# A transformer block with spline weights: gate and up products from 48 features per sorted row group instead of 256-sample rows

## The chip, the cores and the metric

One core of one Trainium2 chip runs the whole program. The metric is the device time of one execution, in microseconds, as the median of several runs. One further execution is taken with the hardware profiler; the figures of the profile are of that one. PE is the matrix engine (PEld its weight loads), DVE the vector engine, ACT the activation engine, POOL the general engine, and SP the engine that issues most of the transfers (DMA); SPq is its queue in the views.

## The reference

Sixteen sequences of 256 tokens with 256 channels go through one pre-norm block: attention with 16 heads of 16, masked so that a token sees no more than 16 tokens ahead, and then a gated feed-forward part with 1024 inner rows. All in float32.

```python
x = x + attn(layernorm(x), wq, wk, wv, wo)
h = layernorm(x)
gate = einsum('bsh,ih->bsi', h, spline(gate_cp, 1024, 256))
up = einsum('bsh,ih->bsi', h, spline(up_cp, 1024, 256))
x = x + einsum('bsi,hi->bsh', silu(gate) * up, spline(down_cp, 256, 1024))
```

`spline` lays 2033 control points evenly over the 262144 entries of the weight in row order and interpolates them with a cubic (Catmull-Rom): each entry is a sum of four neighbouring control points with factors that are a cubic in its place between two knots. A knot comes about every 129 entries, so a half row of 128 entries holds at most one knot: on each side of it the entries are one cubic.

## The kernel before

The kernel is a software pipeline over the 16 sequences. Its outer loop (`for s in range(B + 4)`, from L790) runs 20 steps; in step s several sequences are in work at once: projections of s+3, maxima of the scores of `nb` = s-1, exponentials and values of `tb` = s-2, output projection and second norm of `ob` = s-3, and the feed-forward part of s-4. The engines are wrapped in `InOrder` (L78), so each engine executes its instructions in the order in which the program writes them. All instructions carry the line of that wrapper, L88, in the profile, so they are told apart by tile name.

A step goes, in program order: `inner` (scores of one group of four heads: into PSUM, exponentials by ACT, row maxima by DVE as `z`, `mx`); `values` of `ob`'s second half (tile `po`, copied by ACT to `au`) and `gather`; a second `inner`; `invert`; projections; `outer`; a third `inner`, `values` of `tb`'s first half; `divide`; a fourth `inner`; `project_o` (py); `stats_f`; `outer`; `norm_f` (xnf); `turn_f`; `turn_max`. The pieces of the feed-forward part of s-4 (`gate_up` 0 to 3, `down` 0 and 1) are put between these by `fill(s, gap)` (L697).

Softmax is divided late. `gather` (L517) sends the sums of exponentials from `au` to `den` (four transfers) and half of the heads to `ac` (four). `invert` (L535) takes the reciprocal on DVE (`rec<-den`), writes it to a DRAM tile `rd`, sends the other half of the heads (four transfers), and reads `rd` back spread over 128 partitions as `rb` (two transfers). `divide` (L551) multiplies `ac` by `rb` on DVE, and `project_o` needs it. `turn_max` (L486) turns the maxima on PE (pm), copies them to `mxT` on ACT and sends them into the query tile `qk` (four transfers) for the scores of the next step. `spread` (L337) sends the projected queries and keys into `qk` (eight transfers), `send_factors` and `spread_factors` (L301, L306) send the norm's factors through DRAM (`ra`, `fa`), `load_x` and `load_xT` load inputs, `down` (L618) sends `out`. Nearly all of these leave from SP, which also takes its work in program order and waits at each transfer for what that transfer needs.

Gate and up weights are dense, turned tiles `gateT` and `upT` (128 x 2 x 1024). They are made in the first four steps by `coefficients` (L648, DVE) and `spline` (L655: four PE products, two ACT copies and two predicated DVE copies for each of six parts; two of these parts are `downT`). `turn_f` (L575) turns the normed `xnf` into `x2T`, with 16 DVE transposes of 32-row blocks, for the first and the last sequence on PE. `gate_up(b, i)` (L599) makes 256 inner rows: per weight 2 x 2 products of 128x128 by 256 tokens, for i = 0 and 3 or 0 and 2 (by step) cut in 32-column pieces. PSUM tiles for these come from the pool `ps_f` with two buffers of one bank, so that gate and up products of one piece are two tiles (`pg`, `pu`). ACT makes tanh of the gate (`th`), DVE does `(th + 1) * gate` and then `inter = th * up`.

Of the kernel before, what the change touches and what calls it, by code (L numbers as in the profile page):

```python
# [11 lines left out]
F32 = mybir.dt.float32  # L12
# [64 lines left out]

class InOrder:  # L78
# [15 lines left out]
def block_kernel(  # L94
# [8 lines left out]
    cps: bass.AP,  # L103
    tab: bass.AP,
# [14 lines left out]
    sbx = ctx.enter_context(tc.tile_pool(name="sbx", bufs=10))  # L119
    dr = ctx.enter_context(tc.tile_pool(name="dr", bufs=2, space=bass.MemoryType.DRAM))  # L120
    ps_s = ctx.enter_context(tc.tile_pool(name="ps_s", bufs=1, space=PSUM))
    ps_f = ctx.enter_context(tc.tile_pool(name="ps_f", bufs=2, space=PSUM))
# [30 lines left out]
    cp_in = sb1.tile([P, 8, S], F32, tag="inter", name="cp_in")  # L153
    cp_in = cp_in.rearrange("p i s -> p (i s)").rearrange("p (w n) -> p w n", n=NPART)
    second_in = const.tile([P, 2, NROW], mybir.dt.uint8, tag="second", name="second_in")
    sp.dma_start(cp_in[:, 0, :], cps[0])
    sp.dma_start(second_in, second)
    load_x(2)

    def load_rest(_):  # L160

        load_x(3)
        sp.dma_start(cp_in[:, 1, :], cps[1])
        load_x(4)
        sp.dma_start(cp_in[:, 2, :], cps[2])
        load_x(5)
        load_weight("o", woT, sp)

# [32 lines left out]
    def constants():  # L201

        for t, n, first in ((mask0, JB, 0), (mask1, S, P)):
            pool.memset(t, 0.0)
            pool.affine_select(
                out=t, in_=t, compare_op=ALU.is_ge, fill=NEG, base=first + LOOK,
                pattern=[[-1, n]], channel_multiplier=1,
            )

    gateT = const.tile([P, 2, INTER], F32, tag="gateT", name="gateT")  # L210
    upT = const.tile([P, 2, INTER], F32, tag="upT", name="upT")
    downT = const.tile([P, 8, DIM], F32, tag="downT", name="downT")


    xns, mxs, aus, aos, recs, x2s, x2Ts = ({} for _ in range(7))
# [70 lines left out]
    def sum_weights(nm):  # L286
        sums[nm] = ps_f.tile([P, DIM], F32, tag="f", name=f"sum{nm}")
        for kc in range(2):
            pe.matmul(
                sums[nm], lhsT=means, rhs=w_in[nm][:, kc, :], start=(kc == 0), stop=(kc == 1)  # L290
            )
# [19 lines left out]
    def project_part(b, i, home="m"):  # L311

        if i == 0:
            qkcs[b] = sb.tile([P, 2, 2, S], F32, tag="qkc", name=f"qkc{b}")
        nm, qkc = "qk"[i], qkcs[b]
        pq = (ps_m if home == "m" else ps_f).tile([P, 2, S], F32, tag=home, name=f"p{nm}{b}")
        for oc in range(2):
            for kc in range(2):
                pe.matmul(
                    pq[:, oc, :],  # L320
                    lhsT=w_in[nm][:, kc, oc * P : (oc + 1) * P],
                    rhs=xTs[b][:, kc, :],
                    start=(kc == 0),
                    stop=(kc == 1),
                )
        if b < RAW:
            act.copy(qkc[:, i], pq)
        else:
            dve.tensor_tensor(
                qkc[:, i], pq, across[b].unsqueeze(1).to_broadcast([P, 2, S]), ALU.mult  # L330
            )

# [14 lines left out]
    def project_v(b, engine=act, chunks=(0, 1), home="m"):  # L347
# [3 lines left out]
        else:  # L351
            pv = (ps_m if home == "m" else ps_f).tile([P, 2, DIM], F32, tag=home, name=f"pv{b}")
# [222 lines left out]
    def turn_f(b):  # L575
        x2Ts[b] = sb.tile([P, 2, S], F32, tag="x2T", name=f"x2T{b}")
        if b in (0, B - 1):

            transposed(x2s.pop(b), x2Ts[b], f"tf{b}")
            return  # L580

        src = x2s.pop(b).rearrange("p c (kc d) -> p c kc d", kc=2)
        dst = x2Ts[b].rearrange("p kc (c t) -> p c kc t", c=2)
        for m in range(0, P, 32):
            for q in range(0, P, 32):
                dve.transpose(
                    dst[m : m + 32, :, :, q : q + 32], src[q : q + 32, :, :, m : m + 32]
                )

    def product(out, lhsT, rhs, start, stop, columns=P):  # L590

        for at in range(0, P, columns):
            pe.matmul(
                out[at : at + columns], lhsT=lhsT[:, at : at + columns], rhs=rhs,
                start=start, stop=stop,
            )


    def gate_up(b, i, columns=P):  # L599
        if i == 0:  # L600
            inters[b] = sb1.tile([P, 8, S], F32, tag="inter", name=f"inter{b}")
        pp = []
        for nm, w in (("g", gateT), ("u", upT)):
            t = ps_f.tile([P, 2, S], F32, tag="f", name=f"p{nm}{b}_{i}")
            for ic in range(2):
                for kc in range(2):
                    at = (2 * i + ic) * P
                    product(
                        t[:, ic, :], w[:, kc, at : at + P], x2Ts[b][:, kc, :], kc == 0, kc == 1,
                        columns,  # L610
                    )
            pp.append(t)
        th = sb.tile([P, 2, S], F32, tag="th", name=f"th{b}_{i}")
        act.activation(th, pp[0], AF.Tanh, scale=0.5)
        dve.scalar_tensor_tensor(th, th, 1.0, pp[0], ALU.add, ALU.mult)
        dve.tensor_tensor(inters[b][:, 2 * i : 2 * i + 2, :], th, pp[1], ALU.mult)

    def down(b, c):  # L618
        inter = inters[b]
        if (b, c) == (B - 1, 1):  # L620

            for n in range(0, DIM, P):
                at = slice(n, n + P)
                pd = ps_f.tile([P, P], F32, tag="f", name=f"pd{b}_{c}_{n}")
# [8 lines left out]
        pd = ps_f.tile([P, DIM], F32, tag="f", name=f"pd{b}_{c}")  # L633
# [14 lines left out]
    def coefficients(w):  # L648

        dve.scalar_tensor_tensor(  # L650
            cp_in[:, w, :], cp_in[:, w, :], 0.5 if w == 2 else 1.0, tab_in[:, 0:NPART],
            ALU.mult, ALU.mult,
        )

    def spline(w, part, home="ffmm"):  # L655
        at = slice(NPART * part, NPART * part + NPART)
        places = tab_in[:, NPART + P * part : NPART + P * part + P]

        pw = [

            tiles[q // 2][:, q % 2, :]
            if tag == "s"
            else (ps_f if tag == "f" else ps_m).tile(
                [P, NPART], F32, tag=tag, name=f"pw{w}_{part}_{q}"
            )
            for q, tag in enumerate(home)
        ]
        for q in range(4):
            rows = slice(32 * q, 32 * q + 32)
            pe.matmul(  # L670
                pw[q], lhsT=places[rows], rhs=cp_in[rows, w, :], start=True, stop=True
            )
        for kc in range(2):
            first, other, where = pw[2 * kc], pw[2 * kc + 1], second_in[:, kc, at]
            if w < 2:
                to = (gateT, upT)[w][:, kc, at]
            else:

                to = downT[:, kc::2, NPART // 4 * part : NPART // 4 * (part + 1)]
                first, other, where = (  # L680
                    t.rearrange("p (o q) -> p q o", q=4) for t in (first, other, where)
                )
            act.copy(to, first)
            dve.copy_predicated(to, where, other)

# [4 lines left out]
    parts = ((0, 0), (1, 0), (0, 1), (1, 1), (2, 0), (2, 1))  # L690

    def keep_running(n):
        run = ps_f.tile([P, 2 * S], F32, tag="f", name="run")
# [3 lines left out]
    def fill(s, gap):  # L697

        if s < B - AHEAD:
            order = (  # L700
                (1, gate_up, 0, 32), (3, gate_up, 1), (4, gate_up, 2, 32), (5, gate_up, 3),
                (6, down, 0), (7, down, 1),
            )
        else:
            order = (
                (1, gate_up, 0, 32), (2, gate_up, 1), (3, gate_up, 2), (4, gate_up, 3, 32),
                (6, down, 0), (7, down, 1),
            )
        for at, stage, *what in order:
# [3 lines left out]


    def part(i, home="ffmm"):
        spline(*parts[i], home)

    early = {
        (0, 1): ((stats_a, 1), (value_ones, 1)),
        (0, 2): (  # L720
            (norm_a, 1), (project_qk, 0), (spread, 0), (load_rest, 0), (coefficients, 0),
        ),
        (0, 4): (
            (turn_a, 1, dve), (project_v, 0, dve, (0, 1), "s"), (stats_a, 2), (norm_a, 2),
            (project_part, 1, 0, "f"), (part, 0, "fmmf"),
# [4 lines left out]
        (1, 2): ((project_part, 2, 0), (coefficients, 1)),  # L730
# [4 lines left out]
        (1, 5): ((part, 1),),  # L735
        (1, 6): ((project_qk, 3),),
        (1, 7): (
            (spread, 3), (stats_a, 4), (stats_a, 5), (part, 2, "ssss"), (norm_a, 4),
# [4 lines left out]
            (project_part, 4, 0), (turn_a, 5), (coefficients, 2), (stats_a, 6),  # L743
            (scores_and_values, 5),
        ),
        (2, 3): ((project_part, 4, 1), (spread, 4), (project_part, 5, 0)),
        (2, 4): ((norm_a, 6),),
        (2, 5): ((project_part, 5, 1),),
        (2, 6): ((project_v, 3, act, (1,)), (project_v, 4)),
        (2, 7): ((part, 3, "ssss"), (part, 4)),  # L750
        (3, 1): ((turn_a, 6),),
        (3, 2): ((project_part, 6, 0), (sum_weights, "q"), (center, "q")),
        (3, 3): (
            (project_part, 6, 1), (sum_weights, "k"), (sum_weights, "v"), (center, "k"),
            (center, "v"),
        ),

        (3, 4): ((spread, 5), (spread, 6)),
        (3, 6): ((project_v, 6), (project_v, 5, act, (0,))),
        (3, 7): ((part, 5, "ssss"), (project_v, 5, act, (1,))),  # L760
    }

    def project(s, gap):
# [3 lines left out]
        for stage, b, at in (  # L767
            (stats_a, pb + 1, 1),
            (project_qk, pb, 2),
            (spread, pb, 2),  # L770
            (send_factors, pb + 1, 2),
            (load_xT, pb + 1, 4),
            (project_v, pb, 6),
# [16 lines left out]
    for s in range(B + 4):  # L790
# [36 lines left out]
        if 0 < ob < B - 1:  # L827
            turn_f(ob)
        fill(s, 6)
        if ob == B - 1:  # L830
            turn_f(ob)
        project(s, 6)
        if tb == B - 1:
            values(tb, 1)
            gather(tb)
        do(turn_max, nb)
        project(s, 7)
        if ob == 0:
            turn_f(ob)
        fill(s, 7)  # L840
# [30 lines left out]
```

## Time and profile before

| | us |
|---|---|
| median of 3 runs (646.12 to 646.79) | 646.13 |
| span of the profiled execution | 643.4 |
| a step with projections (s = 4 to 12) | 37.6 |
| a step without (s = 13 to 16) | 32.5 |
| the last three steps together | 80.4 |

| engine operation, tile | count | busy us | mean ns of one |
|---|---|---|---|
| PE products pg and pu | 2560 records | 245.5 | 380 |
| PE products pd | 528 | 117.4 | 376 |
| PE products scores | 4096 | 106.1 | 317 |
| DVE maxima z, with the read of the accumulator | 512 + 512 | 154.4 + 42.7 | 363 + 83 |
| DVE stream transposes x2T | 224 | 67.8 | 303 |
| DVE th and inter | 64 + 64 | 44.0 + 44.0 | 688 |
| ACT tanh th | 64 | 38.3 | 598 |

The span of the profile is the time from the first to the last instruction; the device time holds 2.7 us more. A float32 product of 128 rows by 256 columns leaves two records on PE, and products on different parts of the array overlap, so the busy time of a group is less than its count times its mean. A step is measured between the first score products of two `inner` calls that follow each other at its beginning.

### The profile page before, as it was taken

How to read it: one execution, taken by the hardware profiler on the slowest of the kernel's cores; microseconds unless marked ns; L12 is line 12 of the kernel's file. 1: busy time of each engine (PE TensorE's matmuls, PEld its weight loads, DVE VectorE, ACT ScalarE, POOL GpSimd, SP SyncE). 2: the span in 40 equal slices, each digit the busy share in tenths (PEclk: the TensorE clock that was granted, in tenths of full speed). 3: DMA queues.
4: the chain of work that ended last, by engine and by line, in shares of the span. 5: the costliest groups of instructions: out<-in, count | busy, mean ns of one | idle time of the engine just before them, and what ended most of it. 6: DMA issues, size and time to landing. Idle time of an engine off the chain costs nothing.

```text
span 643.4 us, 21632 instructions
## 1 busy us (share of the span) xinstructions
PE 631.0 (98%) x8876; PEld 466.7 (73%) x8876; DVE 441.0 (69%) x1710; ACT 207.0 (32%) x368; POOL 129.8 (20%) x255
## 2 busy tenths in 40 slices
PE   8999979999999999999999999999999999999998
PEld 7576747777778777777877777787777777776776
DVE  6885746776766777676877767686878787746432
ACT  1355533223232323323232232324232333332110
POOL 4343212112121221211122121111212121212000
PEclk9999989999999999999999999999999999999999
DMA  5832342214140221413123131301010101010100
GB/s 176 181 64 37 72 72 69 37 46 83 36 90 13 82 41 44 85 35 81 21 81 46 42 70 34 67 2 54 3 54 3 54 4 53 3 53 6 48 17 17
DMA packets 40770, 33.39 MB, mean 52 GB/s; under 512 B 10592, under 2 KB 40032, under 8 KB 40672
## 3 DMA queue, kind: packets, MB, share of 16 engines
q1 hardware_dynamic: 39392, 30.90, 21.6%
q8 instruction: 70, 1.15, 0.9%
q10 hardware_dynamic: 1280, 1.11, 0.6%
q14 instruction: 28, 0.23, 0.2%
HBM read 14.42 MB, written 4.47 MB: 29 GB/s over the span
## 4 chain that ended last, share of the span: by engine, by line
PE 86%; DVE 3%; another core or an unknown queue 1%; issue 0%; ACT 0%; DMA 0%; SPq 0%; POOL 0%; ACTq 0%; DVEq 0%
PE pg L88 18%; PE pu L88 17%; PE pd L88 15%; PE scores L88 14%; PE po L88 6%; PE py L88 5%; PE pv L88 3%; PE pk L88 3%; PE pq L88 3%; DVE x2T L88 1%; PE pm L88 1%; DVE z L88 0%; DVE xnf L88 0%; DMA qk<-mxT 0%
## 5 line engine op out<-in xcount | busy, mean ns | idle before, releaser
L88 ACT ACTIVATE e<-scores 128x512 f32<-128x512 f32 (+1 forms) x192 | 117.3, 616 | 269.7 <-PE scores L88 176.9
L88 DVE CUSTOM_DVE_ANT_0 z<-scores,mask 128x144 bf16<-128x144 f32 (+1 forms) x512 | 154.4, 363 | 51.7 <-PE scores L88 37.9
L88 POOL TENSOR_SCALAR_AFFINE_SELECT e<-e 128x224 f32<-128x224 f32 (+1 forms) x192 | 94.0, 490 | 393.6 <-ACT e L88 392.9
L88 PE MATMUL pg<-x2T,gateT 128*32 128x256 f32 (+1 forms) x1280 | 123.9, 381 | 0.6 <-DVE x L88 0.6
L88 PE MATMUL pu<-x2T,upT 128*32 128x256 f32 (+1 forms) x1280 | 121.6, 379 | 0.0
L88 PE MATMUL pd<-downT,inter 128*128 128x256 f32 (+1 forms) x528 | 117.4, 376 | 0.0
L88 PE MATMUL scores<-qk 17*64 17x144 f32 (+7 forms) x4096 | 106.1, 317 | 3.0 <-DVE mx L88 0.9
L88 PEld LDWEIGHTS pd<-downT,inter 128*128 128x128 f32 x528 | 95.6, 190 | 13.6 <-issue 0.4
L88 PEld LDWEIGHTS pu<-x2T,upT 128*32 128x32 f32 (+1 forms) x1280 | 81.9, 126 | 28.6
L88 PEld LDWEIGHTS pg<-x2T,gateT 128*32 128x32 f32 (+1 forms) x1280 | 79.2, 126 | 29.0 <-DVE th L88 1.9
L88 PEld LDWEIGHTS scores<-qk 17*64 17x64 f32 (+1 forms) x4096 | 69.4, 131 | 39.7 <-issue 28.5
L88 DVE SCALAR_TENSOR_TENSOR th<-th,pg 128x512 f32<-128x512 f32 x64 | 44.0, 688 | 68.5 <-ACT th L88 68.5
L88 DVE STREAM_TRANSPOSE x2T<-xnf 32x128 f32<-32x128 f32 x224 | 67.8, 303 | 3.3
L88 ACT ACTIVATE th<-pg 128x512 f32<-128x512 f32 x64 | 38.3, 598 | 76.2 <-PE pg L88 75.6
L88 DVE TENSOR_TENSOR inter<-th,pu 128x512 f32<-128x512 f32 x64 | 44.0, 688 | 25.9 <-PE pu L88 25.9
L88 PE MATMUL po<-e,v 128*32 128x256 f32 (+1 forms) x1024 | 50.0, 336 | 0.0
L88 PEld LDWEIGHTS po<-e,v 128*32 128x32 f32 x1024 | 29.5, 109 | 23.2 <-issue 11.5
L88 DVE DVE_READ_ACCUMULATOR2_ANT mx<- 128x1 f32 x512 | 42.7, 83 | 0.0
L88 PE MATMUL pq<-xT,wq 128*128 128x256 f32 x128 | 31.7, 391 | 0.5 <-ACT xT L88 0.5
L88 PE MATMUL py<-wo,ac 128*128 128x256 f32 x128 | 31.9, 392 | 0.0
L88 PE MATMUL pk<-xT,wk 128*128 128x256 f32 x128 | 30.7, 382 | 0.0
L88 PE MATMUL pv<-wv,xT 128*128 128x256 f32 x120 | 29.8, 391 | 0.0
(81 smaller groups left out, 375.8 us busy)
## 6 DMA issues: line engine op xcount, KB each, us to landing
qk<-qkc SPq DMA_DIRECT2D x124, 64.0 KB
x<-x SPq DMA_DIRECT2D x16, 256.0 KB
ac<-au SPq DMA_DIRECT2D x128, 32.0 KB
rb<-rd SPq DMA_DIRECT2D x32, 128.0 KB
out<-x SPq DMA_DIRECT2D x15, 256.0 KB
xT<-xT SPq DMA_DIRECT2D x9, 256.0 KB
fa<-ra SPq DMA_DIRECT2D x9, 128.0 KB
qk<-mxT SPq DMA_DIRECT2D x64, 4.0 KB
```

The source lines that it names most:

```text
L88: return self.tc.keep_in_program_order(fn(*args, **kwargs))
```

## The change

A half row of 128 samples with one knot in it needs no 128 products. The 1024 inner rows are sorted into eight groups of 128 rows by where their knots lie: in group g the knot of each half row lies among the 16 samples from 16g to 16g+15. Left of these 16 and right of them, the weights of a half row are one cubic each. So a group's product with the tokens needs, for each of the two half rows, 16 single samples of the normed activation and 2 x 4 moments (sums of the activation times powers 0 to 3 of the place, left and right): 48 features, kept in 64 rows of which 16 are zero. Two groups share the 128 partitions of `feat`: 4 x 128 rows of 256 tokens. The weights `gate_w` then are 64 rows by 128 columns for each group, gate and up.

What becomes of the code:

- `turn_f` turns `xnf` on PE for every sequence (four `ptf` transposes and one ACT copy) and stands after the last `outer` and before `turn_max`.
- The new `features(b)` is called at the end of the step: two PE products with the moments table (`pn`), an ACT copy into the third part of `x2T`, and 16 transfers on SP into `feat`. `feat` and `x2T` have one buffer each.
- `gate_up(b, j)` makes two groups: four products with 64 rows each, gate and up of both groups, into one PSUM tile `fb` of two banks which all of `gate_up`, `down`, and the sums share in place of the two buffers of `ps_f`. Gate 0 moves from gap 1 to gap 2; `down` 1 to gap 8, after `turn_max`.
- `gate_w` is made by POOL: `weights(i)` for eight slices in steps 2 and 3, from eight `taps` loads of 384 KB. The four gate and up parts of `spline` and two `coefficients` go.
- Because the inner rows are sorted, `downT` has to be dealt out in the new order: `deal` writes it to DRAM (`turned`) and reads it back in 16 transfers, on SP at the end of step 3.
- For later sequences the first half of the projections moves to gap 1, `project_v` from gap 6 to gap 3.

```diff
+GROUPS, WIDTH, MOMENTS = 8, 16, 8
+ROWS = INTER // GROUPS
...
-    ps_f = ctx.enter_context(tc.tile_pool(name="ps_f", bufs=2, space=PSUM))
+    ps_f = ctx.enter_context(tc.tile_pool(name="ps_f", bufs=1, space=PSUM))
...
+    def load_taps(i):
+        tap_in[i] = sbg.tile([P, 3, 4, HB], F32, tag="taps", name=f"taps{i}")
+        sp.dma_start(tap_in[i], taps[i])
+
+    def weights(i):
+        cp = tap_in[i][:, 1:3]
+        by = tap_in.pop(i)[:, 0].unsqueeze(1).to_broadcast([P, 2, 4, HB])
+        pool.tensor_tensor(cp, cp, by, ALU.mult)
+        pool.tensor_tensor(cp[:, :, 0:2], cp[:, :, 0:2], cp[:, :, 2:4], ALU.add)
+        pool.tensor_tensor(
+            gate_w[:, i // 2, :, HB * (i % 2) : HB * (i % 2) + HB], cp[:, :, 0], cp[:, :, 1],
+            ALU.add,
+        )
+        if i + 2 < 8:
+            load_taps(i + 2)
...
-    gateT = const.tile([P, 2, INTER], F32, tag="gateT", name="gateT")
-    upT = const.tile([P, 2, INTER], F32, tag="upT", name="upT")
+    feat = const.tile([P, 4, S], F32, tag="feat", name="feat")
+    gate_w = const.tile([P, 4, 2, ROWS], F32, tag="gate_w", name="gate_w")
...
+    fb = ps_f.tile([P, 2, 512], F32, tag="f", name="fb")
...
     def turn_f(b):
-        x2Ts[b] = sb.tile([P, 2, S], F32, tag="x2T", name=f"x2T{b}")
-        if b in (0, B - 1):
-            transposed(x2s.pop(b), x2Ts[b], f"tf{b}")
-            return
...
+        x2Ts[b] = sb1.tile([P, 3, S], F32, tag="x2T", name=f"x2T{b}")
+        transposed(x2s.pop(b), x2Ts[b][:, 0:2, :], f"tf{b}")
+
+    def features(b):
+        x2T = x2Ts.pop(b)
+        n = GROUPS * MOMENTS
+        pn = ps_m.tile([P, S], F32, tag="m", name=f"pn{b}")
+        for kc in range(2):
+            pe.matmul(
+                pn[n * kc : n * kc + n], lhsT=mom, rhs=x2T[:, kc, :], start=True, stop=True
+            )
+        act.copy(x2T[:, 2, :], pn)
+        for j in range(4):
+            for kc in range(2):
+                sp.dma_start(feat[kc::4, j, :], x2T[32 * j : 32 * j + 32, kc, :])
+            for kc in range(2):
+                of = n * kc + 16 * j
+                sp.dma_start(feat[2 + 4 * kc :: 8, j, :], x2T[of : of + 16, 2, :])
+
+    def gate_up(b, j):
+        if j == 0:
+            inters[b] = sb1.tile([P, GROUPS, S], F32, tag="inter", name=f"inter{b}")
+        for w in range(2):
+            for half in range(2):
+                rows = slice(HB * half, HB * half + HB)
+                pe.matmul(
+                    fb[:, half, S * w : S * w + S],
+                    lhsT=gate_w[rows, j, w, :], rhs=feat[rows, j, :],
+                    start=True, stop=True,
                 )
...
+        gate, up = fb[:, :, 0:S], fb[:, :, S : 2 * S]
+        th = sb.tile([P, 2, S], F32, tag="th", name=f"th{b}_{j}")
+        act.activation(th, gate, AF.Tanh, scale=0.5)
+        dve.scalar_tensor_tensor(th, th, 1.0, gate, ALU.add, ALU.mult)
+        dve.tensor_tensor(inters[b][:, 2 * j : 2 * j + 2, :], th, up, ALU.mult)
...
+    def deal():
+        turned = dr.tile([2, 8, 8, 8, DIM], F32, tag="turned", name="turned")
+        sp.dma_start(turned.rearrange("o g r k h -> (o g r) (k h)"), down_in[0].rearrange("p k h -> p (k h)"))
+        for odd in range(2):
+            for k in range(8):
+                at = HB * odd + 8 * k
+                sp.dma_start(
+                    downT[at : at + 8], turned[odd, :, :, k, :].rearrange("g r h -> r g h")
+                )
...
     def fill(s, gap):
-        if s < B - AHEAD:
-            order = (
-                (1, gate_up, 0, 32), (3, gate_up, 1), (4, gate_up, 2, 32), (5, gate_up, 3),
-                (6, down, 0), (7, down, 1),
-            )
...
+        for at, stage, *what in (
+            (2, gate_up, 0), (3, gate_up, 1), (4, gate_up, 2), (5, gate_up, 3), (6, down, 0),
+            (8, down, 1),
+        ):
...
         (1, 7): (
-            (spread, 3), (stats_a, 4), (stats_a, 5), (part, 2, "ssss"), (norm_a, 4),
+            (spread, 3), (load_taps, 0), (load_taps, 1), (stats_a, 4), (stats_a, 5), (norm_a, 4),
...
-        (3, 7): ((part, 5, "ssss"), (project_v, 5, act, (1,))),
+        (3, 7): ((spline, 1), (project_v, 5, act, (1,)), (deal,)),
...
-            (project_qk, pb, 2),
+            (first_part, pb, 1),
+            (second_part, pb, 2),
             (spread, pb, 2),
             (send_factors, pb + 1, 2),
+            (project_v, pb, 3),
             (load_xT, pb + 1, 4),
-            (project_v, pb, 6),
...
         do(norm_f, ob)
-        if 0 < ob < B - 1:
-            turn_f(ob)
         fill(s, 6)
-        if ob == B - 1:
-            turn_f(ob)
         project(s, 6)
         if tb == B - 1:
             values(tb, 1)
             gather(tb)
+        do(turn_f, ob)
         do(turn_max, nb)
         project(s, 7)
-        if ob == 0:
-            turn_f(ob)
-        fill(s, 7)
+        fill(s, 8)
+        do(features, ob)
```

## The prediction

> **What bounds the kernel now.** First the page: the share of busy time and the chain that ended last. Then the stretches of three steps of the outer loop, for the price of a step; then the DMA queue of SP through one step.
>
> ```profile
> PE 631.0 (98%) x8876; PEld 466.7 (73%) x8876; DVE 441.0 (69%) x1710; ACT 207.0 (32%) x368; POOL 129.8 (20%) x255
> ...
> PE 86%; DVE 3%; another core or an unknown queue 1%; issue 0%; ACT 0%; DMA 0%; SPq 0%; POOL 0%; ACTq 0%; DVEq 0%
> PE pg L88 18%; PE pu L88 17%; PE pd L88 15%; PE scores L88 14%; PE po L88 6%; PE py L88 5%; PE pv L88 3%; PE pk L88 3%; PE pq L88 3%; DVE x2T L88 1%; PE pm L88 1%; DVE z L88 0%; DVE xnf L88 0%; DMA qk<-mxT 0%
> ```
>
> PE is never idle; gate and up (pg, pu) are the largest part of the chain. SP and DMA have no share in it.
>
> ```profile
> 357.90:395.50 37.60, 37.60 (x547) 28.29 (x546) 27.46 (x108) 11.86 (x21) 7.33 (x14) 1.00 0.25 50
> 465.70:498.20 32.50, 32.50 (x529) 23.73 (x528) 24.71 (x101) 11.06 (x19) 6.60 (x13) 1.00 0.10 28
> 563.00:643.40 80.40, 76.97 (x837) 56.64 (x836) 34.69 (x75) 15.81 (x28) 6.87 (x14) 1.00 0.10 29
> ```
>
> Columns: length, then busy PE, weight loads, DVE, ACT, POOL. A step with projections (s=4 to 12) takes 37.6 us, one without (13 to 16) 32.5, the last three 80.4; DVE is busy 27.5 and 24.7 in a step.
>
> ```profile
> 355.47 2.32 SPq L88 DMA_DIRECT2D qk<-mxT  x4
> 357.89 0.39 SPq L88 DMA_DIRECT2D fa<-ra  x1
> 358.49 0.38 SPq L88 DMA_DIRECT2D out<-x  x1
> 358.93 3.40 SPq L88 DMA_DIRECT2D den<-au  x4
> 362.43 2.63 SPq L88 DMA_DIRECT2D ac<-au  x4
> 367.00 0.49 SPq L88 DMA_DIRECT2D rd<-rec  x1
> 367.54 2.93 SPq L88 DMA_DIRECT2D ac<-au  x4
> 370.59 1.34 SPq L88 DMA_DIRECT2D rb<-rd  x2
> 372.02 6.16 SPq L88 DMA_DIRECT2D qk<-qkc  x8
> 378.28 0.54 SPq L88 DMA_DIRECT2D ra<-rstda  x1
> 378.86 0.46 SPq L88 DMA_DIRECT2D xT<-xT  x1
> ```
>
> Start, length, transfer, of SP alone in one step (its first score matmul at 357.94, called T). Issuing costs SP 0.4 to 0.77 us a transfer however small, and these make about 21 us of 37.6. `den` leaves right at T, `rec` (DVE) runs at T+8.5 without having waited, `rb` leaves at T+12.7, and `ac<-ac,rb` (divide) at T+17.8. All of it lies under PE.
>
> **What goes from PE.** Per sequence 16 groups of pg/pu, at 1.73 us each eight records in the chain (1.92 where a weight load opens it), make 8 pieces: about 14.5 us a step. Added on PE: 16 matmuls with 64 rows, two at a time on the two halves of the rows. The nearest row is `scores<-cp_in`, four 32-row matmuls of 512 columns in 1.14 us, where four one after the other would be 4 x 2 x 0.43 = 3.4; so row halves overlap, and a `gate_up` of four matmuls lies between 0.87 (pairs wholly overlapped) and 1.73 (not at all). I take 0.9, nearer the row that overlaps. Four `ptf` transposes 0.65 and `pn` 0.45 (two 256-column matmuls side by side; 0.87 if not). PE work per step falls to 37.6 - 14.5 + 3.6 + 1.1 = 27.8, and 22.7 late. DVE loses 16 stream transposes (5.0 us). ACT gains two copies (0.59 + 0.38), POOL nothing after step 3. By these engines alone the kernel would gain nearly 10 us a step.
>
> **What comes to SP.** `features` adds 16 transfers for each sequence, 8 of 32 rows and 8 of 16 rows of 1 KB. In SP's order they stand after `mxT`, `fa` and `out` of the old step and ahead of `den`, `ac`, `rd`, `rb` of the new one. SBUF-to-SBUF transfers show these pitches: mxT (2.32 - 0.52)/3 = 0.60, ac 0.68, qk<-qkc 0.77; the shortest one itself is 0.50. The feature copies are one row per partition like mxT: I take 0.60, bounds 0.50 and 0.77: 16 x 0.60 = 9.6 us. The Trainium skill (DMA: Bandwidth & Descriptors, Issuing engines are not separate DMA queues) calls the issue time usually small against the DMA itself; taken at its word the 9.6 would be nothing and the time that of the first rival below. Its Rules for kernel authors there want small transfers coalesced, which speaks against 16 of 16 or 32 KB. The pitch above is the row, so I price by it.
>
> Nothing behind `den` can be had earlier, and DVE executes `rec` in order, after the maxima of the second `inner` and ahead of `qkc`, gate 0 and all of `outer`. So the cover (DVE arrives at T+8.5 and `den` is long there) is gone. Landings:
>
> ```profile
> 91.86 2.30 SPq L88 DMA_DIRECT2D qk<-mxT  x4
> ...
> 94.06 0.56 PEld L88 LDWEIGHTS scores<-qk 17*64 17x64 f32 x24 [1.16 <-DMA qk<-mxT]
> ...
> 603.09 1.33 SPq L88 DMA_DIRECT2D rb<-rd  x2
> ...
> 606.91 0.69 DVE L88 TENSOR_TENSOR ac<-ac,rb 128x512 f32<-128x512 f32 x1 [0.38 <-DMA rb<-rd]
> ```
>
> The scores needed the first mxT transfer alone: issued by 92.38, there at 94.06, 1.7 us. rb needs 606.91 - 604.42 = 2.5 us. For den I take 1.4 (late in the trace `rec` starts 1.4 after den's issue, unwaited; so 1.4 at most).
>
> A step with projections then runs: `out` to T+0.45, features to T+10.05, den 2.4 to T+12.45, landing T+13.85, rec to T+14.4. SP is still issuing ac to T+15.1; rd to 15.6, four ac to 18.1, rb to 19.5, there at T+22.0 (was under 17.8). Meanwhile DVE: qkc 0.7, gate 0 1.4, outer's eight maxima 1.85 to T+18.35. PE has been idle since pv, about T+11, till gate 0 frees the one `fb` at T+16.5. What a pause of PE costs the trace shows:
>
> ```profile
> 35.79 1.14 PE L88 MATMUL scores<-cp_in,tab_in 32*128 32x512 f32 x8
> ...
> 88.17 0.39 PE L88 MATMUL pm<-ident,mx 128*16 128x128 f32 x2 [3.92 <-ACT v L88]
> 88.48 2.05 PE L88 MATMUL scores<-cp_in,tab_in 32*128 32x512 f32 x8
> ```
>
> After 3.9 us of idleness the same eight matmuls took 2.05 instead of 1.14 (granted clock 0.95 over that stretch). So gate 1 and the third `inner` run at about half clock: gate 1 to 18.6, tanh and two DVE operations to 20.65, maxima to 22.1, divide 22.1 to 22.8. Then, DVE and PE by turns over the single `fb`: gate 2 done 25.75, fourth inner's maxima 27.15, x+py and stats 29.2, gate 3 30.6, maxima 32.45, xnf 33.5; PE down 30.95 to 34.6 (3.65), ptf, pm 35.5, second down 39.15, pn 39.6. So the step is 39.6 in place of 37.65: the 14.5 us that PE lost is wait now. Without projections only qkc (0.7) leaves this path: 38.9 in place of 32.45.
>
> **Sum.** Steps 5 to 12: 8 x 1.95 = 15.6. Steps 13 to 16: 4 x 6.45 = 25.8. Step 4 in addition follows `deal`: `turned` (1 MB, about 6 us at the 176 GB/s of the page's first slices), 16 `downT` transfers 9.6 and its own issue, all ahead of features: den about 17.6 later, so 39.6 + 17.6 - 37.4 = 19.8 (bounds 10 and 26 by the transfer rate and pitch). Start: four splines' PE (1.1 to 1.9 each) go, but step 3 already ends on SP's mxT (the wait at 94.06), and taps and POOL's weights come in (POOL's 512-column select takes 0.64; three products per slice perhaps 2, hidden under a POOL busy 20%, and if not hidden, up to 1 us each): -2, bounds -5 and +4. Last three steps: the 17th as the late ones without maxima, 38.7; the 18th has den early, but rd behind features (to +10.1): rd 10.6, ac 13.1, rb 14.4, there at 16.9, then py at half clock to 21.5, x and stats 23.5, gate 3 24.9, xnf 25.7, and two downs, ptf and pn to 33.7; the 19th: first features there at +4.4, four gates in series at 3.6 (PE, tanh 0.6, DVE 1.4, return 0.4), two downs 7.3, out 2.6: 29.5. 101.9 against 80.4: +21.5. Together 15.6 + 25.8 + 19.8 - 2 + 21.5 = 80.7 on a span of 643.4, 724; the median of the runs is 2.7 above the span, so 727.
>
> **Rivals.** *Features hidden, PE the bound*: gate work leaves and nothing waits; 13 steps at -9.7, the last three at -8 each, start -3: 643.4 - 153, with the 2.7 some 493. For it: PE's 86% of the chain. Against: `rec` would have to be ready where DVE arrives, near T+7, so 16 transfers in 2.8 us, a pitch of 0.17 that no row shows. Fifteen steps have features on the path, so the whole change breaks even where 15 x 16 x (0.60 - p) = 81, at p = 0.26; under that it is faster, half the shortest transfer that the trace has. *Deeper stall*: pauses keep PE at half clock after the divide too, or gates don't overlap in pairs (0.87 more each, three on the path). PE's 17 us after rec at half clock in part, some 4 us a step over 15: 787. For it: idleness recurs each step and PE would be busy about 70%. Against: DVE, not PE, paces most of that stretch. *A wash*: no bubbles after rec; then DVE's 16.5 us follow it back to back and a step is 37.0, late 36.3: 8 x -0.65 + 4 x 3.85, with step 4 at 10, the tail at 10 and the start at -5, is +25, so 671. For it: DVE is the engine in line most of that time. Against: every gate needs PE, ACT and DVE in turn over one `fb`. To get to 646 the pitch must fall to its 0.50 besides.
>
> **Chances.** Forecast (685 to 755) 0.70; deeper stall 0.15; wash 0.07; features hidden or nearly 0.08. Nothing less than 0.2% can be told from no change. Range 670 to 765: the lower end takes in the wash, the upper is the forecast with a pitch of 0.68 (1.3 us a step, +19), step 4 and start at their high bounds (+12) and a part of the unpaired gates. Slower 0.89, same 0.02, faster 0.09.
>
> **What would show it.** Right: SP's queue with 16 feat transfers at 0.6 ahead of den; `rec` waiting for DMA den some 5 to 6 us in each step, a chain shared between SPq, DMA, DVE and PE, steps of 38 to 40 us alike before and after step 13, clock under 1. Wrong: rec unwaited, feat pitch well under 0.5, steps under 30, or PE still over 90% busy.

## The result, and the profile after

| | before | after |
|---|---|---|
| median, us | 646.12 (644.28 to 646.79) | 770.42 (762.76 to 770.86) |
| ratio to before, 95% interval | | 1.190 (1.184 to 1.195) |
| span of the profiled execution, us | 643.4 | 769.1 |
| mean of steps 5 to 12, us | 37.7 | 41.8 |
| mean of steps 13 to 16, us | 32.3 | 40.8 |

The changed kernel is slower by 124 us; 81 were forecast, and 770 lies above the range (670 to 765). The lines of the page of after that answer to those of before are the busy time of the engines, the granted clock in 40 slices, and the chain that ended last, by engine and by tile:

```profile
PE 569.4 (74%) x6916; PEld 393.2 (51%) x6916; DVE 360.6 (47%) x1476; ACT 215.4 (28%) x390; POOL 145.9 (19%) x280
...
PEclk9997975797979799797979797969687887887677
...
PE 45%; SPq 19%; DVE 17%; DMA 9%; issue 4%; ACT 3%; POOL 2%; another core or an unknown queue 0%; DVEq 0%; POOLq 0%; ACTq 0%
PE fb L134 24%; SPq L134 19%; PE scores L134 7%; PE po L134 6%; DVE inter L134 4%; DVE th L134 4%; DMA den<-au 3%; DVE z L134 3%; PE pq L134 2%; PE pk L134 2%; DMA downT<-turned 2%; DVE statsf L134 1%; DVE x L134 1%; DMA taps<-taps 1%; ACT th L134 1%
```

No single engine bounds the kernel any more. PE had 86% of the chain and has 45%; SP's queue, which had none, has 19%, and DVE 17%. PE and DVE together are busy 142 us less (61.6 and 80.4), and the kernel takes 124 us more. The stretches of a step with projections, one without, and the last three steps (columns as before; the eighth is the granted clock):

```profile
331.30:371.60 40.30, 32.74 (x428) 22.76 (x426) 22.02 (x91) 12.67 (x23) 6.95 (x14) 0.87 0.28 61
534.90:577.20 42.30, 29.55 (x404) 20.08 (x402) 19.55 (x84) 11.94 (x21) 6.25 (x13) 0.76 0.11 30
657.90:769.00 111.10, 64.57 (x470) 44.11 (x468) 27.14 (x52) 17.49 (x32) 7.06 (x14) 0.74 0.11 31
```

With and without projections a step now takes nearly the same time: what the projections cost PE no longer counts. The busy time of PE (32.74 of 40.30) is swollen by a clock of 0.87. The DMA queue of SP through that first step (start, length, transfer), whose first score product (T) starts at 332.15, and two operations of DVE in it:

```profile
328.75 2.28 SPq L134 DMA_DIRECT2D qk<-mxT  x4
331.13 0.38 SPq L134 DMA_DIRECT2D fa<-ra  x1
332.13 0.38 SPq L134 DMA_DIRECT2D out<-x  x1
332.56 10.59 SPq L134 DMA_DIRECT2D feat<-x2T  x16
343.19 2.46 SPq L134 DMA_DIRECT2D den<-au  x4
345.70 2.65 SPq L134 DMA_DIRECT2D ac<-au  x4
348.45 0.54 SPq L134 DMA_DIRECT2D rd<-rec  x1
349.03 2.51 SPq L134 DMA_DIRECT2D ac<-au  x4
351.63 1.32 SPq L134 DMA_DIRECT2D rb<-rd  x2
...
346.86 0.55 DVE L134 RECIPROCAL rec<-den 64x64 f32<-64x64 f32 x1 [7.54 <-DMA den<-au]
...
355.73 0.69 DVE L134 TENSOR_TENSOR ac<-ac,rb 128x512 f32<-128x512 f32 x1 [0.78 <-DMA x<-x]
```

The 16 feature transfers stand where the prediction put them. `den` leaves 11 us after T instead of right at it, and the reciprocal, which had never waited, waits 7.5 us. Over the whole run, from the waits of DVE (us in total, times, longest):

```profile
DVE rec L134 <- DMA den<-au: 123.2, 14, 15.0
```

In size this is what the kernel lost; whether it is the cause, the experiments have to show. What the pause does to PE in the same step:

```profile
341.57 1.99 PE L134 MATMUL pv<-wv,xT 128*128 128x256 f32 x8
349.31 2.08 PE L134 MATMUL fb<-feat,gate_w 64*128 64x256 f32 x8 [5.75 <-DVE inter L134]
351.32 1.85 PE L134 MATMUL scores<-qk 16*64 16x208 f32 x32
353.10 2.90 PE L134 MATMUL po<-e,v 128*32 128x256 f32 x32
355.93 1.24 PE L134 MATMUL fb<-feat,gate_w 64*128 64x256 f32 x8
357.10 1.04 PE L134 MATMUL scores<-qk 16*64 16x208 f32 x32
...
364.01 3.72 PE L134 MATMUL fb<-downT,inter 128*128 128x256 f32 x16 [1.81 <-DVE inter L134]
```

After 5.75 us of idleness a gate takes 2.08 us and 32 score products 1.85; later in the step the same ones take about 1.13 (1.24 for the first of them) and 1.04. The first `down`, at full clock, takes 3.72.

Where the 125.7 us between the spans lie, stage by stage, each stage measured from one first `qk<-mxT` issue to the next:

| stage | forecast | measured |
|---|---|---|
| start, to the end of step 3 | -2 | +9.9 |
| step 4 | +19.8 | +18.5 |
| steps 5 to 12 | +15.6 | +33.0 |
| steps 13 to 16 | +25.8 | +33.8 |
| the rest | +21.5 | +30.5 |

### The profile page after: what moved, and what is told of

Same layout as the page of the kernel before. It is cut to its first block, busy times and chain, and to the rows that moved or that the text cites. A ratio compares the mean times of both kernels' runs of the same rounds, so it can differ in the third digit from the quotient of the medians.

```text
span 769.1 us, 17911 instructions
## 1 busy us (share of the span) xinstructions
PE 569.4 (74%) x6916; PEld 393.2 (51%) x6916; DVE 360.6 (47%) x1476; ACT 215.4 (28%) x390; POOL 145.9 (19%) x280
## 4 chain that ended last, share of the span: by engine, by line
PE 45%; SPq 19%; DVE 17%; DMA 9%; issue 4%; ACT 3%; POOL 2%; another core or an unknown queue 0%; DVEq 0%; POOLq 0%; ACTq 0%
PE fb L134 24%; SPq L134 19%; PE scores L134 7%; PE po L134 6%; DVE inter L134 4%; DVE th L134 4%; DMA den<-au 3%; DVE z L134 3%; PE pq L134 2%; PE pk L134 2%; DMA downT<-turned 2%; DVE statsf L134 1%; DVE x L134 1%; DMA taps<-taps 1%; ACT th L134 1%
## 5 line engine op out<-in xcount | busy, mean ns | idle before, releaser
L134 PE MATMUL fb<-feat,gate_w 64*128 64x256 f32 x512 | 97.7, 513 | 138.5 <-DVE inter L134 103.9
L134 PE MATMUL fb<-downT,inter 128*128 128x256 f32 (+1 forms) x528 | 126.5, 395 | 32.1 <-DVE inter L134 26.0
L134 PEld LDWEIGHTS fb<-feat,gate_w 64*128 64x128 f32 x512 | 58.6, 246 | 170.2 <-DVE inter L134 122.7
L134 PE MATMUL scores<-qk 17*64 17x144 f32 (+7 forms) x4096 | 121.8, 347 | 13.7 <-DMA qk<-mxT 6.6
L134 PEld LDWEIGHTS fb<-downT,inter 128*128 128x128 f32 x528 | 100.7, 200 | 51.6 <-DVE inter L134 29.2
L134 PEld LDWEIGHTS scores<-qk 17*64 17x64 f32 (+1 forms) x4096 | 75.9, 142 | 57.2 <-issue 19.5
L134 DVE SCALAR_TENSOR_TENSOR th<-th,fb 128x512 f32<-128x512 f32 x64 | 43.4, 677 | 61.0 <-ACT th L134 61.0
L134 PE MATMUL po<-e,v 128*32 128x256 f32 (+1 forms) x1024 | 71.3, 438 | 0.0
L134 DVE RECIPROCAL rec<-den 64x64 f32<-64x64 f32 x16 | 8.7, 544 | 123.2 <-DMA den<-au 123.2
L134 ACT ACTIVATE th<-fb 128x512 f32<-128x512 f32 x64 | 38.3, 599 | 83.6 <-PE fb L134 83.5
L134 PEld LDWEIGHTS po<-e,v 128*32 128x32 f32 x1024 | 36.9, 139 | 39.7 <-issue 32.4
L134 DVE TENSOR_TENSOR inter<-th,fb 128x512 f32<-128x512 f32 x64 | 44.0, 687 | 2.2
L134 PEld LDWEIGHTS py<-wo,ac 128*128 128x128 f32 x128 | 24.1, 198 | 13.7 <-issue 8.9
```

The costliest lines, as they stand in the source:

```text
L134: return self.tc.keep_in_program_order(fn(*args, **kwargs))
```

## The experiments

Unless an interval is given, each is one execution with a profile, beside the kernel before at 645 to 646 us. The end of step 3 lies between 98.7 and 101.8 us in runs whose start is the same program, so differences under 3 us there say nothing in a single run. Of a whole single run the same holds for some 8 us: the four runs of the changed kernel lie between 762.8 and 770.9.

**1 and 2. No features sent, and half of them.** The loop of 16 transfers is taken out, or run for half of the groups.

```diff
-        for j in range(4):
+        for j in range(2):
             for kc in range(2):
                 sp.dma_start(feat[kc::4, j, :], x2T[32 * j : 32 * j + 32, kc, :])
...
```

> The 16 transfers of features are left out, everything else stays (the gate products then read zeros). Theory, SP's queue: rec no longer waits for den (123 us of waiting in the changed kernel), a step falls from 41 to 28 to 31 us, and the time to 540 to 600 us. Rival, the single fb with its turns of PE, ACT and DVE is what makes the step long: the time stays above 690 us.

> Only the transfers for j = 0 and 1 are made, 8 in place of 16. Theory, SP's queue: den leaves 5.4 us earlier in each of 15 steps, so 770 - 81 = 690 us, and some 10 to 20 less if the pauses of PE get short enough for its clock, 670 to 690. Rival, the wait is for the data of a transfer and not for the queue: 750 or more.

Measured: 634.6 without, 682.5 with half, where 670 to 690 was expected. So the 16 transfers cost 136 us, 9 a step: the first eight 48, the other eight 88, or 0.37 and 0.69 us each, spread over 16 sequences. The wait of `rec` for `den` goes the same way: 123.2 us in all, 48.2 with half, 6.1 without. The first few transfers use slack that `rec` had; from then on each costs its full pitch. That settles the main step of the theory. But 634.6 is far above the 540 to 600 expected. Two stretches of the kernel without transfers, with and without projections, and the waits of PE for `inter` in the whole run (us in total, times, longest):

```profile
350.00:382.00 32.00, 29.86 (x428) 21.67 (x427) 21.96 (x91) 12.47 (x23) 7.34 (x14) 1.00 0.28 57
510.60:541.50 30.90, 25.57 (x404) 17.70 (x404) 19.52 (x84) 11.83 (x21) 6.26 (x13) 0.94 0.11 29
...
PE fb L134 <- DVE inter L134: 49.5, 27, 3.6
```

Steps 5 to 12 take 33.0 us in the mean where PE's work had been put at 27.8, and 13 to 16 take 30.9, only 1.5 under before. Most of that is PE's own work, which had been put too low: PE is busy 29.86 of the 32.00 us in the first stretch, at full clock, and 246.0 of the 263.8 us of steps 5 to 12, 30.7 a step. Four gates at 1.13 us, not 0.9, are 0.9 of the difference. What is left, 2.2 us a step, is nearly all waits for `inter` (15.6 us in these eight steps): the pieces of the feed-forward part go round PE, ACT and DVE over the one tile `fb` (experiment 11 shortens one of these turns). Without projections PE is busy 26.0 us of 30.9, where 22.7 had been forecast, and these waits weigh more. With the rest of the change as it is, features that cost nothing would have bought 12 us, not the 153 of the first rival.

**3. Features behind rb.** The transfers are sent a step later, right after `invert`; gates move to gaps 4, 5, 6 and 6, the downs to 8.

```diff
+    def send_features(b):
+        x2T = x2Ts.pop(b)
...
         do(invert, ob)
+        do(send_features, ob - 1)
```

> All 16 transfers, issued a step later, behind rb in SP's order, and the gates put at later gaps. Theory: rec and divide run where they did before the change, without waiting; the gates now wait for feat instead, up to some T+25; a step of 33 to 37 us, 640 to 710 us in all. Rival, 16 more transfers cost their issue time wherever they stand (the queue is full): no change, 750 to 780.

Measured: 815.4, beyond both. The waits of this kernel (us in total, times, longest):

```profile
ACT th L134 <- PE fb L134: 191.8, 51, 10.5
...
PE fb L134 <- DMA feat<-x2T: 60.8, 16, 8.8
```

`rec` waits for `den` only once (6.1 us), as the theory had it. But now the first gate waits 3.8 us a sequence for features, and the gates, which the same edit moved to the end of the step, run there one after the other with both downs behind them. How much each of the two costs, this run doesn't say. Placing 16 transfers elsewhere in the queue moved the wait; it didn't take it away.

**4. Five transfers in place of 16.** At the same place, `x2T` is written once to DRAM and read back by four transfers.

```diff
+        d = dr.tile([P, 3, S], F32, tag="fd", name=f"fd{b}")
+        sp.dma_start(d, x2T)
+        for kc in range(2):
+            sp.dma_start(feat[kc::4], d[:, kc, :].rearrange("(j q) t -> q j t", j=4))
...
```

> The same features through DRAM: one transfer out and four in, in place of 16, at the same place in the order. Theory, the count of transfers: 5 x 0.6 and one landing of about 2 us are 5 us in place of 10.9, so as with half the transfers 670 to 700 us. Rival, the bytes or the landing decide: the bytes double, 760 or more.

Measured: 708.2, 62 less than after, and a little above the expected 670 to 700. The queue of SP in one step:

```profile
309.56 0.35 SPq L134 DMA_DIRECT2D fd<-x2T  x1
312.79 2.63 SPq L134 DMA_DIRECT2D feat<-fd  x4
```

Five transfers carry the same rows in 3.0 us of issue instead of 10.6. But SP stands still for 2.9 us between them, since the reads wait till the write has landed. `rec` waits 59.7 us for `den` in all, 63.5 less than in the changed kernel, about as much as the time fell. The price was one of issues, not of bytes: here still more bytes are moved, and through DRAM.

**5. The reads behind den.** As in 4, with the write in two parts and the four reads issued after `den`.

```diff
         recs[b] = den
+        if b - 1 in fd:
+            read_features(b - 1)
```

> Through DRAM as before (one transfer out in two parts, four in), but the four in stand behind den in SP's order. Theory: den leaves at the start of the step again, rec no longer waits, and steps come to what they are without any transfers of features, 33 and 31 us, or 1 to 2 more: 635 to 665 us. Rival, the wait moves to the gates, which now get feat later: 690 or more, with PE waiting for feat.

Measured: 698.7, as the rival had it. `rec` no longer waits, but PE does, and again pays with its clock:

```profile
307.62 1.14 PE L134 MATMUL fb<-feat,gate_w 64*128 64x256 f32 x8 [1.66 <-DMA feat<-fd]
308.69 1.58 PE L134 MATMUL scores<-qk 16*64 16x80 f32 x64
310.20 3.08 PE L134 MATMUL pv<-wv,xT 128*128 128x256 f32 x8
...
325.00 5.41 PE L134 MATMUL fb<-downT,inter 128*128 128x256 f32 x16 [1.94 <-DVE inter L134]
```

`pv` takes 3.08 instead of 1.99 and a down 5.41 instead of 3.72, after pauses of under 2 us. In all, PE waits 69.9 us for `feat` in this run. Issuing the features from another engine than SP was not tried.

**6 and 9. Keeping PE busy through the wait.** In 6, 12 products into a spare tile go ahead of gate 1; in 9, 11 products go into the tile of `pv` ahead of the real ones, in steps 4 to 12.

```diff
+        if b >= RAW:
+            for _ in range(11):
+                pe.matmul(
+                    pv[:, 0, :], lhsT=xTs[b][:, 0, 0:P], rhs=w_in["v"][:, 0, :],
+                    start=True, stop=True,
+                )
```

> The changed kernel with 12 products more in each of steps 4 to 16, put where PE pauses for gate 1 (they write a PSUM tile that nobody reads). Theory, half clock after the pause is part of the path: gate 1, inner and po run in 1.1, 1.0 and 1.5 us in place of 2.1, 1.85 and 2.9, and 1.5 to 3 us a step come back: 730 to 752 us. Rival, DVE alone paces that stretch: no change, 762 to 772.

> The changed kernel with 11 products more in each of steps 4 to 12, into pv's own tile ahead of its real products, so that PE works through the pause instead of standing. (The 12 of the run before stood behind a PSUM buffer that came free only after the pause.) Theory, half clock after the pause is part of the path: gate 1, inner and po in 1.1, 1.0 and 1.5 us, and steps 5 to 12 fall from 41.8 on average to 38.5 to 40.5; the time by 10 to 25 us. Rival, DVE alone paces that stretch: steps stay at 41 to 42.

Measured: 795.7 and 760.5. In 6 the spare tile came free only with `qkc`, after the pause, so the products lengthened the wait instead of filling it; that run says nothing of the question, beyond gates at 1.13 after them. In 9 they filled it:

```profile
330.12 6.74 PE L134 MATMUL pv<-wv,xT 128*128 128x256 f32 x30
338.12 1.13 PE L134 MATMUL fb<-feat,gate_w 64*128 64x256 f32 x8 [1.26 <-DVE inter L134]
...
352.03 5.27 PE L134 MATMUL fb<-downT,inter 128*128 128x256 f32 x16 [1.87 <-DVE inter L134]
...
340.44 1.32 SPq L134 DMA_DIRECT2D rb<-rd  x2
...
345.27 0.69 DVE L134 TENSOR_TENSOR ac<-ac,rb 128x512 f32<-128x512 f32 x1 [1.50 <-DMA x<-x]
```

Gate 1 is back at 1.13, and yet steps 5 to 12 go from 41.8 only to 41.0 (38.5 to 40.5 was expected). Not even these 0.8 us are sure: in 7 and 8 the same steps, with no product added, take 41.0 and 41.3. The divide still waits 1.5 us for a transfer (the view names `x<-x`, which was issued right behind `rb`), so the half clock of gate 1 and the third `inner` lay under SP's chain; and the clock falls later instead, in the first down (5.27). In the steps, half clock is a small part of the loss.

**7. Taps a stage later.** The load of taps i+1 is issued at `weights(i)`, not that of i+2 after it.

```diff
+        if 0 < i < 7:
+            load_taps(i + 1)
         cp = tap_in[i][:, 1:3]
...
-        if i + 2 < 8:
-            load_taps(i + 2)
```

> Each load of taps is issued one stage later, when POOL has long finished with the buffer, so SP does not stand waiting for POOL. Theory: the maxima of sequence 1 leave at 62 in place of 66.8 us and all after it moves by 4 to 6 us. Rival, POOL's eight slices themselves hold up the exponentials' masks: under 2 us.

Measured: 769.0, no gain in the whole, as the rival had it. By steps it shows more. Step 2 takes 24.4 us instead of 28.3 (23.8 before), so the wait behind the taps was what step 2 had lost, as the theory had it. Step 3 takes 39.7 instead of 34.9 and gives it back; POOL waits there three times for taps that now come late (4.1, 3.8 and 6.7 us). What the start loses is told below.

**8. No deal.** One transfer fills `downT`, whose rows then stand in the old order.

```diff
-        turned = dr.tile([2, 8, 8, 8, DIM], F32, tag="turned", name="turned")
...
+        sp.dma_start(downT, down_in[0])
```

> downT is filled by one transfer from down_in and keeps the old order of rows; turned and its 16 transfers are left out. Theory: step 4 falls by the 14 to 17 us for which these stand ahead of features, from 56 to 39 to 42 us, and nothing else changes. Rival, step 4 is long because of something else that comes with the first sequence (cold PE, first features): it stays above 50.

Measured: 755.6, and step 4 takes 41.1 us instead of 55.9. The 14.8 us are `deal` alone (17.6 forecast, though the items listed there, 6, 9.6 and an issue, give some 16); without it step 4 is a step like the others.

**10, 11 and 12. Versions built on these readings.** 10: features through DRAM with six transfers (the write in two parts, as in 5); `pn` goes ahead of the second down, so that the write and its landing lie under that down and the reads are out before `den`; taps a stage later; `deal` writes in step 3 and reads in step 4 behind `rb`. 11: also gate 3 ahead of `stats_f`, so that PE doesn't wait for that turn. 12: also the order of SP's transfers from `den` on is two `ac`, `rd`, four `ac`, `rb`, two `ac`.

```diff
         project(s, 7)
-        fill(s, 8)
         do(features, ob)
+        do(read_features, ob)
+        fill(s, 8)
...
         do(project_o, ob)
+        fill(s, 5)
         do(stats_f, ob)
         project(s, 5)
-        fill(s, 5)
...
-        gather_heads(b, 0)
+        gather_heads(b, 0, (0, 1))
```

> The features through DRAM, with pn ahead of the second down so that the parts land under it and are read back before den; taps a stage later; downT dealt out in step 4 behind rb. Theory: the transfers of features lie under work, a step comes to 33 to 35 us with projections and 31 to 33 without, step 4 to some 40: 610 to 650 us. Rival, the turns over fb and the half clock keep a step at 36 and more: 665 to 695.

> As the one before, with gate 3 ahead of the second norm's statistics in DVE's order. Theory: the first down no longer waits 1.8 us for gate 3, so 0.8 to 1.2 us a step less, 12 to 18 us in all than the one before. Rival, the norm comes later by as much and ptf waits instead: within 5 us of it.

> The same kernel as the one before it in this study (features through DRAM, gate 3 ahead of the statistics), with the order of SP's transfers between den and rb changed: two ac transfers, rd, four ac, rb, two ac, in place of four ac, rd, four ac, rb. The work is the same; rb leaves about 1.3 us earlier. Theory (the chain den, rec, rd, rb on SP still sets the divide, and through a late divide the two steps of 35.3 us in which py runs at half clock): the two long steps fall to about 32, most others lose 0 to 0.6, the divide no longer waits for a transfer: 621 to 628 us. Rival (in most steps the divide follows the fourth inner's maxima without waiting, and the long steps come from elsewhere): 629 to 635 us, long steps remain. Against the kernel before: a ratio of 0.96 to 0.97 by the theory, 0.975 to 0.985 by the rival.

| | median, us | ratio to before, 95% interval |
|---|---|---|
| 10 (8 runs) | 646.6 (641.0 to 653.2) | 0.999 (0.995 to 1.004) |
| 11 (2 runs) | 632.3 (631.7 to 632.9) | 0.979 (0.972 to 0.987) |
| 12 (6 runs) | 637.1 (630.9 to 640.8) | 0.983 (0.979 to 0.987) |

10 takes the whole loss back and is not to be told from before; its steps 5 to 12 take 34.7 us, as the theory had it. 11 is faster than before by 2%, with these steps at 33.0 us, as without any feature transfers, though there gate 3 still stood later. PE is busy 243.9 of the 264.1 us of these steps (92%), so there it is close to being the bound again. The page of 11 and its queue in one step:

```profile
PE 533.1 (85%) x6916; PEld 374.5 (59%) x6916; DVE 360.5 (57%) x1476; ACT 213.2 (34%) x390; POOL 146.7 (23%) x280
...
235.75 0.43 SPq L134 DMA_DIRECT2D fd<-x2T  x1
236.29 3.95 SPq L134 DMA_DIRECT2D feat<-fd  x4
240.34 0.53 SPq L134 DMA_DIRECT2D out<-x  x1
240.91 2.36 SPq L134 DMA_DIRECT2D den<-au  x4
```

`den` is out 10.4 us after `mxT` was begun, in the changed kernel 16.9. 12 can't be told from 11, and 637.1 lies above both ranges that were expected for it. `rb` does leave earlier, but the divide then waits for the `ac` transfers, which come last; steps 5 to 12 fall from 33.0 to 32.6, and step 4, where the 16 reads of `deal` follow, takes 48.5 instead of 39.3:

```profile
DVE ac L134 <- DMA ac<-au: 10.7, 10, 2.3
```

## Why the prediction had the right cause and too small a size

**What goes from PE: right in kind, too large in worth.** A gate of four products takes 1.13 us at full clock (0.9 taken, bounds 0.87 and 1.73). That PE's work falls was right. That by the engines alone nearly 10 us a step would be gained was not: without any transfer the step fell by 4.7 us (37.7 to 33.0), late steps by 1.5. The first rival (493 us) took steps of 27.8 and 22.7 us from PE's work alone. PE is busy 30.7 and 26.0 us in them, and the turns over `fb` add waits. This hardly touched the forecast, which took the turns one by one.

**Features ahead of den: right, and the mis-sized term in the steps.** In the mean of steps 5 to 12, after T: features issued by 11.4 (10.05 forecast), `rec` begun at 15.1 (13.85), `rb` issued by 21.2 (19.5), divide at 24.1 (22.1), step 41.8 (39.6). So 1.35 of the 2.2 us come with the features, 0.4 between `den` and `rb`, 0.3 between the issue of `rb` and the divide (2.9 instead of 2.6), and 0.2 after the divide. The pitch was 0.66 to 0.73 us, 0.69 in the mean, not 0.60: the row taken was `mxT`, and the upper end of the range had 0.68 with 1.3 us a step, which is about what came. The landing of `den`, 1.2 us from the end of its issue (345.65 to 346.86 in the lines above) against 1.4, was priced well.

Three of the eight steps take 42.8 to 43.8 us, the five others 40.3 to 41.3: one has a pause of 3.7 us on DVE that the trace ascribes to nothing it names, in one `rb` came late, in one a down ran at half clock. Such long steps differ between executions: with the same steps, 7 and 8 have a mean of 41.0 and 41.3, so up to 0.8 of the 2.2 belongs to this execution. Steps 13 to 16 miss by about the same, 2.0 each, as the forecast's "alike before and after step 13" says.

**Half clock: right after rec, mis-sized in the tail.** Gate 1 and the third `inner` run at half clock as forecast (2.08, 1.85). Experiment 9 shows that this lies under SP's chain. In the last step, though, the forecast took four gates in series at 3.6 each, which is at full clock. They come at 4.2 (743.42 to 747.64), and the first `down` begins at half clock too:

```profile
743.42 2.08 PE L134 MATMUL fb<-feat,gate_w 64*128 64x256 f32 x8 [2.13 <-DVE inter L134]
747.64 2.08 PE L134 MATMUL fb<-feat,gate_w 64*128 64x256 f32 x8 [2.14 <-DVE inter L134]
751.86 2.08 PE L134 MATMUL fb<-feat,gate_w 64*128 64x256 f32 x8 [2.14 <-DVE inter L134]
756.08 5.13 PE L134 MATMUL fb<-downT,inter 128*128 128x256 f32 x16 [2.14 <-DVE inter L134]
```

PE works half of this time only, and the granted clock is 0.50 from 738.5 to 758.9; it is back at 1.00 only within that `down`. The gates and the `down` are 3.9 us over their price by this. The last three steps are 111.1 us (101.9 forecast); from the end of one `pn` to that of the next they take 40.1, 36.2 and 34.0, where 38.7, 33.7 and 29.5 were forecast. So half clock explains most of the miss of the last step; three of the four gates of the step before it came at half clock as well (2.08 each). This is the second rival's mechanism, in the place where the forecast had left it out.

**Step 4: right.** +18.5 against +19.8; experiment 8 gives `deal` 14.8 of it.

**Start: wrong in sign.** -2 was forecast, with +4 as the upper bound; +9.9 came. The step that failed is that of POOL's weights "hidden under a POOL busy 20%". The lines of step 2, from the timeline:

```profile
56.62 10.10 SPq L134 DMA_DIRECT2D taps<-taps  x4
66.82 2.27 SPq L134 DMA_DIRECT2D qk<-mxT  x4
...
63.77 2.07 POOL L134 TENSOR_TENSOR taps<-taps 128x512 f32<-128x512 f32 x2
65.92 0.45 POOL L134 TENSOR_TENSOR gate_w<-taps 128x128 f32<-128x128 f32 x1
...
60.82 0.38 PE L134 MATMUL pm<-ident,mx 128*16 128x128 f32 x2
...
69.49 1.82 PE L134 MATMUL scores<-qk 17*64 17x208 f32 x24 [4.60 <-DMA qk<-mxT]
71.24 2.90 PE L134 MATMUL po<-e,v 128*32 128x256 f32 x32
```

`pm` is ready at 61.2, but `mxT` leaves at 66.82. Ahead of it in SP's order stand four taps loads. A load waits till POOL is through with the buffer that it fills: the last two wait 6.0 us for that, and SP stands 10.1 us at four transfers. PE then idles 4.6 us and starts step 3 at half clock. The price of POOL's work was nearly right (2.5 us a slice; 2 had been taken), its place was not: it was costed on POOL, where it was hidden, and not on SP, where the next load waits for it. It is the same kind of error that the prediction had avoided with the features. Of the 9.9 us, 4.5 fall in step 2 and 3.4 in step 3; the other 2.0 are within the spread between runs. The 4.5 are the taps: with the loads a stage later, in 7 and in 10 to 12, step 2 takes 23.9 to 24.4 us (23.8 before). The 3.4 of step 3 are there with these later loads too (33.9 to 35.2 in 10 to 12, 31.5 before); their cause stays open.

**The sum.** Misses of 11.9 (start), 17.4 and 8.0 (steps), 9.0 (tail), less 1.3 (step 4), are the 45 us between the span forecast and the span measured. The upper end of the range had 19 us for a longer pitch in all steps (steps 5 to 16 alone missed by 25), 6 for the start (it missed by 12) and nothing for half clock in the last step (the tail missed by 9); these three put the time above it.

## What to carry to other kernels

Price a small transfer by its issue and by what stands behind it in its queue, not by its bytes: 16 of them cost 9 us a step here, and six that move more bytes, placed under other work, cost some 1.7 by one run each (34.7 us a step in 10, 33.0 without any). Before work is taken from the engine that bounds a kernel, write down what else ends where that engine ends; the second bound, not the saved work, tells the gain; here that was what PE still had to do, 30.7 us a step and not 27.8. Of a load that waits for a buffer, ask who is queued behind it on the issuing engine.

## What the runs showed of the hardware

An issue on SP did not take longer with more bytes: one feature transfer of 16 or 32 KB took 0.49 to 1.49 us (median 0.59), the write of 384 KB in experiment 4 0.35. The Trainium skill (DMA: Bandwidth & Descriptors, Issuing engines are not separate DMA queues) calls the time to initiate a transfer usually small against the transfer. Here it was not: 0.59 us for a feature transfer stand beside the 1.2 us after the end of its issue in which `den`, also a small transfer, had landed, and 16 of them kept SP for 10.6 us of a step. Its Rules for kernel authors, which ask for coalescing small transfers, agree with experiment 4 (62 us less).

The clock fell after short pauses, too. The Trainium skill (TensorE: Matmul & The Clock Gate, Why this matters for your kernels) warns of idle gaps of more than about 3 us. The runs show half clock after 5.75 us, but also a down of 5.27 and 5.41 us (3.72 at full clock) after single pauses of 1.87 and 1.94, and four gates of 2.08 in the last step with pauses of 2.13 to 2.14 between them. Why about the same pause ahead of the first down sometimes leaves the clock alone (1.81 us, then 3.72, in the step shown above; 1.78 us, then 5.41, in the step before it) is open.
